# The head of a four-layer image kernel: moments of all samples in one run, weights loaded last and squared on GpSimd, bias sums under the last transpose, constant products on TensorE

## The chip, the cores and the metric

The kernel runs on one NeuronCore of a Trainium2 chip. The metric is device time in microseconds (us) of one execution; less is better. Below, PE is TensorE, DVE is VectorE, ACT is ScalarE, POOL is GpSimd, and SP is the engine whose queue issues most transfers. Everything is float32.

## The reference, cut to what matters

The input is four images of 56x56 pixels with 128 channels. Four layers follow one another, each as `x = x + layer(group_norm(x))`. The first layer is window attention followed by global attention and an MLP; the others (edge sums, a Fourier layer with attention, a convolution) are not touched here.

```
def _gn(v, G=32, eps=1e-5):
    ...
    m = jnp.mean(g, axis=(1, 2, 4), keepdims=True)
    s = jnp.var(g, axis=(1, 2, 4), keepdims=True)
    return ((g - m) / jnp.sqrt(s + eps)).reshape(v.shape)
...
x = x + _L0_conv_ref(_gn(x), L0_conv_wq, L0_conv_bq, ...)
```

Inside the first layer, attention is `softmax(q k / sqrt(32)) v`. A softmax needs the row's maximum only if scores can be large. The kernel therefore computes, before anything else, an upper bound for all scores from the longest normalized token and the norms of the weights' columns. If the bound is small, it takes a fast path without maxima; otherwise a general path. With the inputs given it takes the fast path.

## The kernel before, in words

Channels lie on the 128 partitions; a sample is a tile of 128x3136 (56x56 tokens), worked on in seven blocks of 448 tokens (`NBLK`, `NB`). This study concerns the head of the program, from the start to the branch `tc.If(small_scores > 0)` (L2868). The rest, some 3450 us, is the same in both versions.

**Loads.** SP issues eight transfers in the order sample 0 (`xw`), the pack `t_shared` (identity and the group matrix `g4`), samples 1 and 2 (`i_x`), the pack `t_first` (the first layer's weights), sample 3, the packs `t_edge` and `t_images` (L2829, L102).

**Moments.** `norm_steps` (L925) is a generator for one sample. Its first seven steps are one `bn_stats` each (L931, DVE). The eighth aggregates them (L934, `i_mv`) and multiplies by `g4` on PE (L936, into `i_ps`) to average over a group of four channels. The next step copies the mean (L940), forms the variance (L941, L942), multiplies by `g4` again (L943) and takes the root on ACT (L944). The last step inverts it on DVE (L946), forms the shift (L947), and squares the whole normalized sample on ACT in one instruction (L949, `i_sq`).

**Lengths.** `measure` inside `input_norms` (L954) multiplies the seven blocks of a sample's squares by a matrix of ones (L972), four blocks to a PSUM bank `i_len` (three banks in rotation), and reduces each full bank to a maximum per partition on DVE (L975, `i_tops`). At the end the maxima are reduced (L993, `i_top`), transposed on PE (L995, `i_pt`) and reduced to one number, `longest` (L996).

**Order.** Scheduling is by hand for PE, ACT and DVE: instructions stand in their queues as the Python code emits them. `input_norms` runs sample b's late steps in between the `bn_stats` of sample b+1, and calls `next(between)` once per sample, which advances a second generator: `score_bounds` (L999), then `attention_bias` (L899), then `edge_weights` (L1337). So `score_bounds` squares the weights `wq` and `wk` on DVE (`z_sq`, L1008 to L1011) and sums the squares' columns on PE (`z_p`, L1012 to L1015), all after sample 2's moments; scales and squares the sums (`z_both`, L1019 on DVE, L1020 on ACT) after sample 3's; and sums them by head (`z_norm`, L1026). `attention_bias` computes products of weights and shifts on PE (`b_p`, L905 to L909 and L920), scaled weights on DVE (`w_fq`, `w_fk`, `w_fv`, `w_f1`, L912), and adds biases (L916 to L922). They all stand ahead of the last sample's products.

**End of the head.** `scores_are_small` (L1031) combines `longest` and the norms into the flag `z_small`, which every engine loads (L1048) before it branches (L2868). Then POOL clears buffers (L339 to L345), ACT and DVE normalize the first groups of sample 0 (`w_xg`, L368 and L193), and PE projects them (L375, L376, L380), the results being copied out by L225, L223, L232, L230 and L383.

Elsewhere in the kernel (L1259, `e_idle`) PE already multiplies constants by constants, with a result that nobody reads.

Of the kernel before, what the change touches and what calls it, by code (L numbers as in the profile page):

```python
# [12 lines left out]
F32 = mybir.dt.float32  # L13
# [7 lines left out]
B = 4  # L21
# [76 lines left out]
def load_pack(k, pool, name, pack, owners):  # L98

    ap, places = pack  # L100
    t = pool.tile(list(ap.shape), F32, name="t_" + name)
    k.nc.sync.dma_start(t, ap)  # L102
    for n, shape, c in places:
        v = t[:shape[0], c:c + math.prod(shape[1:])]
        if len(shape) > 2:
            dims = ["d%d" % i for i in range(1, len(shape))]
            v = v.rearrange("p (%s) -> p %s" % (" ".join(dims), " ".join(dims)), **dict(zip(dims, shape[1:])))
        for prefix, owner in owners:
            if n.startswith(prefix):
                setattr(owner, n[len(prefix):], v)  # L110
# [788 lines left out]
def attention_bias(k, w, pool):  # L899


    nc = k.nc
    with k.tc.tile_pool(name="b_ps", bufs=1, space=PSUM) as psum:
        ps = psum.tile([P, 512], F32, name="b_p")
        nc.tensor.matmul(ps[:, 0:1], w.wo, w.bv, start=True, stop=True)  # L905
        for i, t in enumerate((w.wq, w.wk, w.wv)):
            nc.tensor.matmul(ps[:, 1 + i:2 + i], t, w.be1, start=True, stop=True)
        for f in range(4):
            nc.tensor.matmul(ps[:, 4 + f:5 + f], w.w1[:, f * P:(f + 1) * P], w.be2, start=True, stop=True)  # L909
        for n, t, g in (("fq", w.wq, w.g1), ("fk", w.wk, w.g1), ("fv", w.wv, w.g1), ("f1", w.w1, w.g2)):  # L910
            f = pool.tile(list(t.shape), F32, name="w_" + n)
            nc.vector.tensor_scalar_mul(f, t, g)  # L912
            setattr(w, n, f)
        for i, (n, bias) in enumerate((("bvo", w.bo), ("fbq", w.bq), ("fbk", w.bk), ("fbv", w.bv))):
            f = pool.tile([P, 1], F32, name="w_" + n)
            nc.vector.tensor_add(f, ps[:, i:i + 1], bias)  # L916
            setattr(w, n, f)
        w.fb1 = pool.tile([P, 4], F32, name="w_fb1")
        nc.vector.tensor_add(w.fb1, ps[:, 4:8], w.b1)
        nc.tensor.matmul(ps[:, 8:9], w.wo, w.fbv, start=True, stop=True)  # L920
        w.fbvo = pool.tile([P, 1], F32, name="w_fbvo")
        nc.vector.tensor_add(w.fbvo, ps[:, 8:9], w.bo)  # L922


def norm_steps(k, x, b, wk, psum):  # L925


    nc = k.nc
    st = wk.tile([P, NBLK, 6], F32, name="i_st")
    for j in range(NBLK):  # L930
        nc.vector.bn_stats(st[:, j, :], x[:, blk(j)])  # L931
        yield
    mv = wk.tile([P, 2], F32, name="i_mv")
    nc.vector.bn_aggr(mv, st.rearrange("p a b -> p (a b)"))  # L934
    ps = psum.tile([P, 512], F32, tag="mm", name="i_ps")
    nc.tensor.matmul(ps[:, 0:1], k.g4, mv[:, 0:1], start=True, stop=True)  # L936
    yield
    mr = k.mr[:, b, :]
    t = wk.tile([P, 2], F32, name="i_t")
    nc.vector.tensor_copy(mr[:, 0:1], ps[:, 0:1])  # L940
    nc.vector.tensor_sub(t[:, 0:1], mv[:, 0:1], mr[:, 0:1])  # L941
    nc.vector.scalar_tensor_tensor(t[:, 0:1], t[:, 0:1], t[:, 0:1], mv[:, 1:2], ALU.mult, ALU.add)  # L942
    nc.tensor.matmul(ps[:, 1:2], k.g4, t[:, 0:1], start=True, stop=True)  # L943
    nc.scalar.activation(t[:, 1:2], ps[:, 1:2], AF.Sqrt, bias=k.eps)  # L944
    yield
    nc.vector.reciprocal(mr[:, 1:2], t[:, 1:2])  # L946
    nc.vector.scalar_tensor_tensor(t[:, 0:1], mr[:, 0:1], -1.0, mr[:, 1:2], ALU.mult, ALU.mult)  # L947
    sq = wk.tile([P, TOK], F32, name="i_sq")
    nc.scalar.activation(sq, x, AF.Square, bias=t[:, 0:1], scale=mr[:, 1:2])  # L949
    k.squares[b] = sq  # L950
    yield


def input_norms(k, x, pool, wk, psum, between):  # L954

    nc = k.nc
    k.mr = pool.tile([P, B, 2], F32, name="mr0")
    k.longest = pool.tile([1, 1], F32, name="longest")  # L960
    k.squares = {}
    tops = wk.tile([P, NBLK], F32, name="i_tops", bufs=1)
    banks = {}

    def measure(b):
        sq = k.squares.pop(b)
        for j in range(NBLK):
            n = NBLK * b + j
            q = n % 4
            if q == 0:  # L970
                banks[n // 4] = psum.tile([P, 512], F32, tag="i_len", name="i_len", bufs=3)
            nc.tensor.matmul(banks[n // 4][32 * q:32 * q + 32, :NB], k.ones[:, 0:32], sq[:, blk(j)],  # L972
                             start=True, stop=True)
            if q == 3:
                nc.vector.tensor_reduce(tops[:, n // 4:n // 4 + 1], banks.pop(n // 4)[:, :NB], AX.X, ALU.max)  # L975

    steps = [norm_steps(k, x[b], b, wk, psum) for b in range(B)]
    for _ in range(NBLK + 1):
        next(steps[0])
    for b in range(B):  # L980
        ahead = steps[b + 1] if b + 1 < B else iter(())
        for n in range(NBLK + 1):
            next(ahead, None)
            if n in (1, 4):
                next(steps[b])
        next(between, None)
        if b:
            measure(b - 1)
    for _ in between:
        pass  # L990
    measure(B - 1)
    top = wk.tile([P, 1], F32, name="i_top", bufs=1)
    nc.vector.tensor_reduce(top, tops, AX.X, ALU.max)  # L993
    pt = psum.tile([P, 512], F32, tag="i_len", name="i_pt", bufs=3)
    nc.tensor.matmul(pt[0:1, :P], top, k.ident, start=True, stop=True)  # L995
    nc.vector.tensor_reduce(k.longest, pt[0:1, :P], AX.X, ALU.max)  # L996


def score_bounds(k, w, bounds, wk, psum, limits=(76.0, 64.0)):  # L999


    nc = k.nc
    ps = psum.tile([1, 2, 2, 2, P], F32, tag="z_p", name="z_p", bufs=1)
    for layer in range(2):
        for i, (wt, bias) in enumerate(((w.wq, w.bq), (w.wk, w.bk))):
            sq = wk.tile([P, P], F32, name="z_sq", bufs=4)
            if layer:
                nc.vector.tensor_scalar_mul(sq, wt, w.g1)  # L1008
                nc.vector.tensor_mul(sq, sq, sq)
            else:  # L1010
                nc.vector.tensor_mul(sq, wt, wt)  # L1011
            nc.tensor.matmul(ps[:, layer, i, 0, :], k.ones[:, 0:1], sq, start=True, stop=True)  # L1012
            if layer:
                nc.tensor.matmul(ps[:, layer, i, 1, :], w.be1, wt, start=True, stop=False)
            nc.tensor.matmul(ps[:, layer, i, 1, :], bias, k.ident, start=not layer, stop=True)  # L1015
    yield
    for layer in range(2):
        both = wk.tile([1, 2, 2, P], F32, name="z_both")
        nc.vector.tensor_scalar_mul(both[:, :, 0, :], ps[:, layer, :, 0, :], float(P) if layer else 1.0)  # L1019
        nc.scalar.activation(both[:, :, 1, :], ps[:, layer, :, 1, :], AF.Square)  # L1020
        bounds.append((both, limits[layer]))
    yield
    for layer in range(2):
        norm = wk.tile([1, 2, 2, 4], F32, name="z_norm%d" % layer, bufs=1)
        both, limit = bounds[layer]
        nc.vector.tensor_reduce(norm, both.rearrange("p i a (h d) -> p i a h d", h=4), AX.X, ALU.add)  # L1026
        bounds[layer] = norm, limit
    yield
# [308 lines left out]
def edge_weights(k, w, pool):  # L1337

    for n, t in (("nW2", w.W2), ("nbn", w.bn)):
        r = pool.tile(list(t.shape), F32, name="e_" + n)  # L1340
        k.nc.vector.tensor_scalar_mul(r, t, -1.0)
        setattr(w, n, r)
# [1455 lines left out]
def build(k, packs, I, out):  # L2798
# [3 lines left out]
    with ExitStack() as es:  # L2802
# [16 lines left out]
        with tc.tile_pool(name="w01", bufs=1) as wp, tc.tile_pool(name="io", bufs=1) as io:  # L2819
            xw = io.tile([P, TOK], F32, name="xw")  # L2820
            with ExitStack() as pre:
# [2 lines left out]
                w0, w1, w2 = Env(), Env(), Env()  # L2824
                owners = (("const_", k), ("in_w0_", w0), ("in_w1_", w1), ("in_w2_", w2))
                for b in range(B):
                    if b == 3:
                        load_pack(k, wp, "first", packs["first"], owners)
                    nc.sync.dma_start(x[b], I["x"][b])  # L2829
                    if b == 0:  # L2830
                        load_pack(k, cp, "shared", packs["shared"], owners)
                load_pack(k, wp, "edge", packs["edge"], owners)
                load_pack(k, l2p, "images", packs["images"], owners)
                make_consts(k, cp)
# [3 lines left out]
                                                              mybir.EngineType.DVE}))  # L2838
                bounds = []

                def between():
                    yield
                    yield from score_bounds(k, w0, bounds, wk, psum)
                    attention_bias(k, w0, wp)
                    edge_weights(k, w1, wp)

                input_norms(k, x, wp, wk, psum, between())
                k.shift = wp.tile([P, B], F32, name="shift0")
                nc.vector.scalar_tensor_tensor(k.shift, k.mr[:, :, 0], -1.0, k.mr[:, :, 1], ALU.mult, ALU.mult)
                small_scores = scores_are_small(k, bounds, wp, wk)  # L2850
# [102 lines left out]
```

## Time and profile before

| | us |
|---|---|
| median of 3 runs | 3492.82 |
| lowest and highest | 3477.65, 3494.12 |
| the profiled execution | 3507.88 |
| its span in the profile | 3505.9 |
| first work after the branch (`w_xg`, L368) begins | 52.92 |

| engine | busy us | share of the span |
|---|---|---|
| PE | 3342.7 | 95% |
| DVE | 2674.1 | 76% |
| ACT | 2130.6 | 61% |
| POOL | 1278.5 | 36% |

The profile is one execution, with a time of its own. A busy PE is not a PE at its peak, since the clock that it is granted varies; the page gives that clock by slice, and a window query gives it for any stretch. In the timeline a row is a start, a duration, an engine, a line of the program, the operation, its output and inputs, how many instructions are merged, and in brackets the idle time before it with what ended it. A float32 matmul shows as two records.

### The profile page before, as it was taken

The numbers are of one execution on the slowest core, as the hardware profiler recorded it, in microseconds if no ns is written. First come the engines' busy times: TensorE is split into PE (matmuls) and PEld (weight loads), VectorE is DVE, ScalarE is ACT, GpSimd is POOL, SyncE is SP. The second block draws the span as 40 slices with busy tenths as digits, with TensorE's granted clock in tenths as the row PEclk, the third lists the DMA queues.
The fourth block names the chain that finished last, engine by engine and source line by source line (L and its number), as shares of the span: only waits on it lengthen the run. The fifth ranks groups of instructions, "written<-read, shape, count | busy, mean of one in ns | idle before, by whom it ended". The sixth has DMA issues, their size and how long they took to land. (4 is left out here: it accounts for less than half of the span.)

```text
span 3505.9 us, 64398 instructions
## 1 busy us (share of the span) xinstructions
PE 3342.7 (95%) x27774; PEld 1447.5 (41%) x27774; DVE 2674.1 (76%) x2563; ACT 2130.6 (61%) x2251; POOL 1278.5 (36%) x784
## 2 busy tenths in 40 slices
PE   6999999999999999999999999999988999999998
PEld 4433333353333435333343543334346433336664
DVE  5588867868888696788859768885975778885766
ACT  4688876668888566788857578886642013215442
POOL 0000007700000590000029200001864778874776
PEclk8999999999999999999999999999998999999999
DMA  2134420023433000534400044332022047743201
GB/s 105 43 88 92 96 53 19 20 59 85 98 88 79 19 1 20 122 89 96 97 24 1 20 96 100 85 85 43 1 104 52 1 95 187 186 105 93 57 18 56
DMA packets 98014, 243.44 MB, mean 69 GB/s; under 512 B 64457, under 2 KB 69833, under 8 KB 92713
## 3 DMA queue, kind: packets, MB, share of 16 engines
q0 software_dynamic: 16128, 102.77, 14.7%
q1 hardware_dynamic: 74872, 123.61, 12.1%
q10 hardware_dynamic: 6720, 12.85, 1.3%
q8 instruction: 221, 3.62, 0.4%
q14 instruction: 73, 0.59, 0.1%
HBM read 79.43 MB, written 31.33 MB: 32 GB/s over the span
## 5 line engine op out<-in xcount | busy, mean ns | idle before, releaser
L830 ACT ACTIVATE f_ring<-f_pm 128x1792 f32<-128x1792 f32 (+1 forms) x764 | 1093.8, 1482 | 226.7 <-PE f_pm L827 179.7
L682 DVE TENSOR_TENSOR f_acc<-f_acc,f_ring 128x1792 f32<-128x1792 f32 x468 | 947.7, 2025 | 191.4 <-ACT f_ring L830 162.0
L827 PE MATMUL f_pm<-f_qT,f_kT 32*128 32x448 f32 x5376 | 723.0, 571 | 9.9 <-ACT f_p L716 4.1
L693 PE MATMUL f_pm<-f_ring,f_va 128*32 128x448 f32 (+1 forms) x6304 | 589.4, 490 | 0.0
L672 POOL DMA_DIRECT2D f_far<-f_ring x112 | 96.6, 862 | 1326.9 <-ACT f_ring L830 1071.8
L1230 POOL TENSOR_TENSOR e_tp<-e_a,e_c 128x1792 f32<-128x1792 f32 (+2 forms) x172 | 480.3, 2844 | 36.9 <-issue 36.9
L1228 DVE TENSOR_TENSOR e_td<-e_a,e_pc 128x1792 f32<-128x1792 f32 (+2 forms) x292 | 478.5, 1707 | 8.8 <-ACT e_c L1216 8.8
L827 PEld LDWEIGHTS f_pm<-f_qT,f_kT 32*128 32x128 f32 x5376 | 260.1, 183 | 412.0 <-ACT f_ring L830 300.8
L693 PEld LDWEIGHTS f_pm<-f_ring,f_va 128*32 128x32 f32 x6304 | 163.8, 109 | 410.1 <-issue 397.8
L1232 ACT ACTIVATE e_tp<-e_tp 128x1792 f32<-128x1792 f32 (+2 forms) x172 | 253.3, 1495 | 97.9 <-POOL e_tp L1230 97.9
L1979 DVE TENSOR_TENSOR u_ud<-u_px,u_d 112x1792 f32<-112x1792 f32 x144 | 263.5, 1864 | 39.8 <-PE u_po L1984 35.5
L1981 POOL TENSOR_TENSOR u_up<-xh,u_d 112x1792 f32<-112x1792 f32 (+1 forms) x72 | 241.0, 3375 | 55.2 <-PE u_po L1984 42.9
L1299 PE MATMUL e_acc<-e_td,t_edge 128*32 128x448 f32 x1952 | 231.6, 542 | 6.6 <-DVE e_td L1228 6.6
L1984 PE MATMUL u_po<-u_ud,AT 112*64 112x448 f32 x1056 | 213.8, 544 | 1.9 <-DVE u_ud L1979 1.9
L1299 PE MATMUL e_acc<-e_tp,t_edge 128*32 128x448 f32 x1184 | 147.9, 543 | 23.6 <-ACT e_tp L1232 23.6
L1984 PEld LDWEIGHTS u_po<-u_ud,AT 112*64 112x64 f32 x1056 | 74.5, 138 | 128.9 <-issue 112.9
L1299 PEld LDWEIGHTS e_acc<-e_td,t_edge 128*32 128x32 f32 x1952 | 61.7, 110 | 142.5 <-issue 93.8
L737 DVE RECIPROCAL f_den<-f_den 128x448 f32<-128x448 f32 x28 | 82.6, 2951 | 45.1 <-ACT f_den L734 45.1
L1823 POOL TENSOR_TENSOR q_u<-iS,q_g 128x1792 f32<-128x1792 f32 x32 | 102.8, 3235 | 28.4 <-PE q_acc L1838 28.4
L1838 PE MATMUL q_acc<-q_u,S 64*64 64x448 f32 x1024 | 106.5, 561 | 4.4 <-DVE q_u L1825 3.3
L813 POOL TENSOR_TENSOR x<-xf,xw 128x343 f32<-128x343 f32 x28 | 25.5, 910 | 226.5 <-DVE xf L802 226.5
L1984 PE MATMUL u_po<-u_up,AT 112*64 112x448 f32 x480 | 104.1, 547 | 2.4 <-POOL u_up L1981 2.4
(522 smaller groups left out, 4550.4 us busy)
## 6 DMA issues: line engine op xcount, KB each, us to landing
f_far<-f_ring POOLq DMA_DIRECT2D x112, 896.0 KB, 6.4
u_d<-dd SPq DMA_DIRECT2D x46, 784.0 KB
f_far<-f_ring SPq DMA_DIRECT2D x28, 896.0 KB
xw<-in_x SPq DMA_DIRECT2D x4, 1568.0 KB
x2d<-x SPq DMA_DIRECT2D x4, 1568.0 KB
xat<-x SPq DMA_DIRECT2D x4, 1568.0 KB
x_xs<-xat ACTq DMA_DIRECT2D x32, 196.0 KB
xm<-x_ev ACTq DMA_DIRECT2D x64, 98.0 KB
```

Source lines behind the costliest of these rows:

```text
L682: nc.vector.tensor_add(e.acc, e.acc, slots(j, c))
L693: nc.tensor.matmul(e.po[heads[h], part], va[o, c, heads[h]], p, start=(c == 0), stop=(c == 23 and part.stop == NB))
L827: nc.tensor.matmul(ss[:, i, :NB], kT[heads[h], c * P:(c + 1) * P], qT[heads[h], blk(j)], start=True, stop=True)
L830: nc.scalar.activation(ring[:, slot:slot + m, :], ss[:, :m, :NB], AF.Exp, scale=scale)
L1228: nc.vector.tensor_tensor(t, am, cm, ALU.max)
L1230: nc.gpsimd.tensor_sub(t, am, cm)
L1232: nc.scalar.activation(tf, tf, AF.Relu)
L1299: nc.tensor.matmul(acc[quarters[r0 + r], :NB], w.S[:, 0, :], t[:, r].rearrange("p l n -> p (l n)"), start=(g == 0), stop=(g == len(turns) ...
L1838: nc.tensor.matmul(acc[bp][i][halves[hb % 2], hb // 2, :NB], x[o], u[o, 8 * hb:8 * hb + 8, :].rearrange("p h t -> p (h t)"), start=first, ...
L1979: nc.vector.tensor_mul(u, bc(px[:, :, :NB], 2, m), dm)
L1981: nc.gpsimd.tensor_mul(u, bc(x, 2, m), dm)
L1984: nc.tensor.matmul(po[64 * b2:64 * b2 + 64, :NB], st.AT[:, 8 * i + h0 + q, 2 * bp + b2, :], u[:, b2, q, :], start=(left == 16), stop=(left ...
```

## The change

- The pack `t_first` is loaded after sample 3.
- `input_norms` no longer calls a generator between samples. The products of sample b-2 (`products`) are emitted inside the moments of sample b, and the reductions of their banks (`longest(b)`) are separate calls. The weights' work comes after sample 3's moments, in an order written out by hand. `z_p` is allocated at the beginning.
- `fill(n)` emits n products of a constant by a constant, 384 wide, into the bank of `z_p`: three inside sample 2's moments, three inside sample 3's, two before sample 3's second product, one after the last products, and four at the end.
- The squares of the weights (`z_sq`), the scaled weights `w_f*` and the squares in `z_both` are computed on POOL. The value that is squared in `z_both` is first copied from PSUM by DVE.
- The square of a sample is two ACT instructions, of four blocks and of three.
- `attention_bias` emits its `b_p` products and `w_f*` after the transpose of `i_top` has been emitted on PE, and its additions (now in `added`) before `longest` is reduced on DVE. Its PSUM pool is left open until then.

```diff
@@ attention_bias
-    with k.tc.tile_pool(name="b_ps", bufs=1, space=PSUM) as psum:
-        ps = psum.tile([P, 512], F32, name="b_p")
+    psum = k.tc.tile_pool(name="b_ps", bufs=1, space=PSUM)
+    ps = psum.__enter__().tile([P, 512], F32, name="b_p")
...
-            nc.vector.tensor_scalar_mul(f, t, g)
+            nc.gpsimd.tensor_scalar_mul(f, t, g)
             setattr(w, n, f)
+
+    def added():
...
+        psum.__exit__(None, None, None)
+
+    return added
@@ norm_steps
-    nc.scalar.activation(sq, x, AF.Square, bias=t[:, 0:1], scale=mr[:, 1:2])
+    for o in (slice(0, 4 * NB), slice(4 * NB, TOK)):
+        nc.scalar.activation(sq[:, o], x[:, o], AF.Square, bias=t[:, 0:1], scale=mr[:, 1:2])
@@ input_norms
+    ps = psum.tile([1, 2, 2, 2, P], F32, tag="z_p", name="z_p", bufs=1)
+
+    def fill(n):
+
+        for _ in range(n):
+            nc.tensor.matmul(ps[:, 0].rearrange("p i a c -> p (i a c)")[:, :3 * P], k.ones[:, 0:1], bc(k.ones, 1, 3),
+                             start=True, stop=True)
 
     steps = [norm_steps(k, x[b], b, wk, psum) for b in range(B)]
+    work = weights(ps)
     for _ in range(NBLK + 1):
         next(steps[0])
-    for b in range(B):
-        ahead = steps[b + 1] if b + 1 < B else iter(())
+    for b in range(1, B):
         for n in range(NBLK + 1):
-            next(ahead, None)
+            next(steps[b])
             if n in (1, 4):
-                next(steps[b])
-        next(between, None)
-        if b:
-            measure(b - 1)
-    for _ in between:
-        pass
-    measure(B - 1)
+                next(steps[b - 1])
+            if n == 5 and b > 1:
+                fill(3)
+                products(b - 2)
+            if n == 5 and b == 3:
+                next(work)
+        if b == 2:
+            longest(0)
+    longest(1)
+    fill(2)
+    next(steps[3])
+    next(steps[3])
+    products(2)
+    longest(2)
+    next(work)
+    next(work)
+    products(3)
+    next(work)
+    longest(3)
     top = wk.tile([P, 1], F32, name="i_top", bufs=1)
     nc.vector.tensor_reduce(top, tops, AX.X, ALU.max)
+    fill(1)
     pt = psum.tile([P, 512], F32, tag="i_len", name="i_pt", bufs=3)
     nc.tensor.matmul(pt[0:1, :P], top, k.ident, start=True, stop=True)
+    for _ in range(2):
+        next(work)
     nc.vector.tensor_reduce(k.longest, pt[0:1, :P], AX.X, ALU.max)
+    fill(4)
@@ score_bounds
-                nc.vector.tensor_scalar_mul(sq, wt, w.g1)
-                nc.vector.tensor_mul(sq, sq, sq)
+                nc.gpsimd.tensor_scalar_mul(sq, wt, w.g1)
+                nc.gpsimd.tensor_mul(sq, sq, sq)
             else:
-                nc.vector.tensor_mul(sq, wt, wt)
+                nc.gpsimd.tensor_mul(sq, wt, wt)
...
-        nc.scalar.activation(both[:, :, 1, :], ps[:, layer, :, 1, :], AF.Square)
+        nc.vector.tensor_copy(both[:, :, 1, :], ps[:, layer, :, 1, :])
+        nc.gpsimd.tensor_mul(both[:, :, 1, :], both[:, :, 1, :], both[:, :, 1, :])
@@ build
                 for b in range(B):
-                    if b == 3:
-                        load_pack(k, wp, "first", packs["first"], owners)
                     nc.sync.dma_start(x[b], I["x"][b])
...
+                load_pack(k, wp, "first", packs["first"], owners)
                 load_pack(k, wp, "edge", packs["edge"], owners)
...
-                def between():
+                def weights(ps):
+                    yield from score_bounds(k, w0, bounds, wk, ps)
+                    added = attention_bias(k, w0, wp)
+                    edge_weights(k, w1, wp)
                     yield
-                    yield from score_bounds(k, w0, bounds, wk, psum)
-                    attention_bias(k, w0, wp)
-                    edge_weights(k, w1, wp)
+                    added()
+                    yield
```

More of the change, by code (lines that the diff above doesn't have):

```diff
@@ L902, in attention_bias @@
     nc = k.nc
-    with k.tc.tile_pool(name="b_ps", bufs=1, space=PSUM) as psum:
-        ps = psum.tile([P, 512], F32, name="b_p")
+    psum = k.tc.tile_pool(name="b_ps", bufs=1, space=PSUM)
+    ps = psum.__enter__().tile([P, 512], F32, name="b_p")
+    if True:
         nc.tensor.matmul(ps[:, 0:1], w.wo, w.bv, start=True, stop=True)
@@ L948, in norm_steps, with input_norms @@
     sq = wk.tile([P, TOK], F32, name="i_sq")
-    nc.scalar.activation(sq, x, AF.Square, bias=t[:, 0:1], scale=mr[:, 1:2])
+    for o in (slice(0, 4 * NB), slice(4 * NB, TOK)):
+        nc.scalar.activation(sq[:, o], x[:, o], AF.Square, bias=t[:, 0:1], scale=mr[:, 1:2])
     k.squares[b] = sq
     yield
-def input_norms(k, x, pool, wk, psum, between):
+def input_norms(k, x, pool, wk, psum, weights):
     nc = k.nc
@@ L963, in input_norms, with products @@
     banks = {}
-    def measure(b):
+    def products(b):
         sq = k.squares.pop(b)
@@ L973, in measure, with longest @@
                              start=True, stop=True)
-            if q == 3:
-                nc.vector.tensor_reduce(tops[:, n // 4:n // 4 + 1], banks.pop(n // 4)[:, :NB], AX.X, ALU.max)
+    def longest(b):
+        for n in range(NBLK * b // 4, (NBLK * b + NBLK) // 4):
+            nc.vector.tensor_reduce(tops[:, n:n + 1], banks.pop(n)[:, :NB], AX.X, ALU.max)
+    ps = psum.tile([1, 2, 2, 2, P], F32, tag="z_p", name="z_p", bufs=1)
[3 more added lines that the diff above has]
+                             start=True, stop=True)
@@ L994, in input_norms, with score_bounds @@
     pt = psum.tile([P, 512], F32, tag="i_len", name="i_pt", bufs=3)
     nc.tensor.matmul(pt[0:1, :P], top, k.ident, start=True, stop=True)
+    for _ in range(2):
+        next(work)
     nc.vector.tensor_reduce(k.longest, pt[0:1, :P], AX.X, ALU.max)
-def score_bounds(k, w, bounds, wk, psum, limits=(76.0, 64.0)):
+    fill(4)
+def score_bounds(k, w, bounds, wk, ps, limits=(76.0, 64.0)):
     nc = k.nc
-    ps = psum.tile([1, 2, 2, 2, P], F32, tag="z_p", name="z_p", bufs=1)
+    squares = []
+    for layer in range(2):
+        for wt in (w.wq, w.wk):
+            sq = wk.tile([P, P], F32, name="z_sq", bufs=4)
+            if layer:
+                nc.gpsimd.tensor_scalar_mul(sq, wt, w.g1)
+                nc.gpsimd.tensor_mul(sq, sq, sq)
+            else:
+                nc.gpsimd.tensor_mul(sq, wt, wt)
+            squares.append(sq)
+    yield
@@ L1004, in score_bounds @@
     for layer in range(2):
         for i, (wt, bias) in enumerate(((w.wq, w.bq), (w.wk, w.bk))):
-            sq = wk.tile([P, P], F32, name="z_sq", bufs=4)
-            if layer:
-                nc.vector.tensor_scalar_mul(sq, wt, w.g1)
-                nc.vector.tensor_mul(sq, sq, sq)
-            else:
-                nc.vector.tensor_mul(sq, wt, wt)
+            sq = squares.pop(0)
             nc.tensor.matmul(ps[:, layer, i, 0, :], k.ones[:, 0:1], sq, start=True, stop=True)
@@ L2839, in build @@
                 bounds = []
-                def between():
+                def weights(ps):
+                    yield from score_bounds(k, w0, bounds, wk, ps)
+                    added = attention_bias(k, w0, wp)
+                    edge_weights(k, w1, wp)
                     yield
-                    yield from score_bounds(k, w0, bounds, wk, psum)
-                    attention_bias(k, w0, wp)
-                    edge_weights(k, w1, wp)
-                input_norms(k, x, wp, wk, psum, between())
+                    added()
+                    yield
+                input_norms(k, x, wp, wk, psum, weights)
                 k.shift = wp.tile([P, B], F32, name="shift0")
```

## The prediction, made before the changed kernel had run

> **What bounds the kernel now.** I read the page's 40 slices first: PE is at 9 nearly throughout, but at 6 in slice 1, and the granted clock dips there to 8. The page's chain explains only some 27% of the span and never reaches the start, so I read the first 53 us in order of time, then the waits, then 2-us windows for the clock.
>
> ```profile
> PE   6999999999999999999999999999988999999998
> PEclk8999999999999999999999999999998999999999
> ```
>
> The program cannot start sample 0 before `z_small` is known and the branch taken. First window work starts at 52.92. Timeline of that stage (start, duration, engine, line):
>
> ```profile
> 21.47 0.42 DVE L1011 TENSOR_TENSOR z_sq<-t_first 128x128 f32<-128x128 f32 x2
> ...
> 26.89 0.63 DVE L975 TENSOR_REDUCE i_tops<-i_len 128x1 f32<-128x448 f32 x1 [3.95 <-PE i_len L972]
> 27.44 1.14 DVE L931 BATCH_NORM_STATS2 i_st<-i_x 128x6 f32<-128x448 f32 x2
> ...
> 38.96 3.00 ACT L949 ACTIVATE i_sq<-i_x,i_t,mr 128x3136 f32<-128x3136 f32 x1 [0.50 <-DVE i_t L947]
> ...
> 42.89 1.85 PE L909 MATMUL b_p<-t_first 128*128 128x1 f32 x8
> ...
> 45.77 3.21 PE L972 MATMUL i_len<-i_sq,c_ones 128*32 128x448 f32 x14
> ...
> 50.41 0.28 DVE L996 TENSOR_REDUCE longest<-i_pt 1x1 f32<-1x128 f32 x1 [0.56 <-PE i_pt L995]
> ...
> 52.92 1.32 ACT L368 ACTIVATE w_xg<-xw,shift,mr 128x392 f32<-128x392 f32 x2 [1.62 <-DVE z_small L1047]
> ```
>
> To see: sample 3's moments (27.44) sit on DVE behind the weights' squares and a reduction that waits 3.95 us for PE; from there the chain is moments 3, square 3 (38.96), `b_p` on PE ahead of the last products, products (45.77), `longest`, branch.
>
> The clock column (seventh; PE's busy time comes first) shows how slowly PE runs here:
>
> ```profile
> 32.00:34.00 2.00, 1.40 (x10) 0.87 (x13) 1.01 (x4) 2.00 (x2) 0.00 (x0) 0.54 0.01 4
> 46.00:48.00 2.00, 2.00 (x11) 0.37 (x6) 0.69 (x4) 0.00 (x0) 0.00 (x0) 0.50 0.00 0
> 50.00:52.00 2.00, 0.38 (x2) 0.08 (x2) 1.20 (x8) 0.32 (x2) 0.00 (x0) 1.00 0.00 0
> 54.00:56.00 2.00, 2.00 (x4) 0.85 (x3) 1.18 (x2) 0.24 (x1) 2.00 (x6) 0.50 0.00 0
> 60.00:62.00 2.00, 2.00 (x26) 1.46 (x26) 1.32 (x4) 0.68 (x3) 1.43 (x7) 1.00 0.00 0
> ```
>
> From 32 to 49 it is half, then again from 53 to 59, when sample 0 starts. Seven products take 3.21 us so; the first set, at 25.68, took 1.88. (At 22 the column says 1.00, but `z_p` pairs come 0.43 apart and after 25.4 only 0.22: it was half until then.)
>
> [...] grants at 25.2, 49.2 and 59.3 follow dense starts at 22.2, 45.8 and 53.7, so 3.1 to 5.6 us. [...]1792 wide: 3.27 against 1.71[...] one-input 448 wide took 1.40 on POOL, 512 wide 0.48 on DVE. [...] Before, that load (L813) lay 28 us ahead of its first use[...].
>
> **The change, part by part.** Until 21.55 (moments 2) DVE, ACT and their DMAs stay as they are.
>
> *Loads.* SP issues as many DMAs, `t_first` third from last. By the windows' GB/s, 7.40 MB have moved at 19.9; the first sample's statistics ran some 1.1 after its last byte, so `t_first` is usable at about 21.0, `t_edge` at 22.8, x3 at 19.0. Users: POOL at 21.0, DVE's `e_nW` after 40. Nothing waits that matters.
>
> *To POOL.* Off DVE go six `z_sq` instructions (1.5 us) and four `w_f*` (1.3); off ACT two squares (0.62). On POOL, from L2062 (112 wide, 0.418), L813 (343, 0.910), L1744 (64, 0.442) and L1715 (448, 1.406): 128-wide two-input 0.45, one-input 0.60, 512-wide 1.57. Squares 4x0.45+2x0.60=3.0, so 21.0 to 24.0[...]; `w_f*` 3.4 more. PE wants `z_sq` at 34.9: [...] later than that, each us is one on the path. `w_f*` is read by L468 at 115. The two `z_both` squares (0.72 each) now pass DVE, POOL, DVE: +0.5 us on the path to the last reductions.
>
> *Constant products.* 3+3+2+1+4=13. `e_idle` at 684.34 (four 384-wide records in 1.45, the last 0.49 long) gives 0.32 a record, 0.64 a matmul at full clock; cold is twice that, as `z_p` shows. So three cost 1.9 to 3.85 us, ahead of the real products and of moments 2 and 3's small matmuls, L942 and L949, in PE's queue. They write the bank of `z_p` before its sums start; only the one after products 3 waits, for `z_both` to be read (37.8 below), and that is past.
>
> *Halved Square.* 1792 wide took 1.70 (L1232), 1344 wide 1.29 (L830): 3.0 together; I charge 0.05. It helps only if PE would wait for sample 3, and by my sum it doesn't.
>
> *Sum.* Fill 18.85 to 22.7, cold. Clock granted between 22.0 and 24.5 (3.1 to 5.6 after start); I take 23.2. Products 0: first bank 24.0, all 24.9. DVE idles from 21.55 for that bank, reduces to 24.7, then two of x3's statistics to 25.9, copy and two small ops to 26.4, three statistics. Before, that triple started at 29.00 and square 2 began 2.05 later, moments 3 were aggregated 3.45 later: now square 2 28.55 to 31.6, moments 3 at 29.95, against 32.45. **2.5 us.** PE: L949 to 27.05, fill to 28.97, products 1 (1.88) to 30.85, L942 to 31.3, fill (2) to 32.6, L949 to 33.0. Square 3 follows by 0.8: 33.85 to 36.9. Before 38.96: **5.1 us**; the gain there is PE at full clock. Products 2 to 34.9, ten `z_p` (0.215) to 37.05, products 3 to 38.95. DVE meanwhile: two reductions to 35.2, `z_both` to 37.8, POOL to 38.6, norms to 39.3, last reductions to 40.55, `i_top` 40.7, against 49.85: **9.1 us**, of which `b_p` (4.6 on PE before) is only postponed.
>
> *`b_p` under the transpose.* `longest` now stands on DVE behind eight instructions, six waiting for `b_p` or its last product. Transpose to 41.2; nine weight loads: eight `b_p` cost 0.46 each cold (1.42 for three), 0.25 at full clock (loads of 128 took 190 ns a record in L1259): 2.0 to 3.7, I take 2.3 as the clock has few products to hold it: 43.5. Adds, L923, `w_fbvo`: 1.26 before, 1.35 here with waits: 44.85. From `longest` to first work took 2.51: 47.4 against 52.92, **5.5 us**. Ends: `b_p` cold and grant late, 49.4, 3.5 us; all early, 46, 7 us.
>
> *Sample 0's start.* Four fills at 44.6 to 47.2 end before L375 (48.2): PE starts at full clock. L375 to L380 took 4.9 us cold, 2.5 at full clock. But evacuations on DVE and ACT (four of 0.6, then two copies) hold most: the copy into `w_vd` comes 1 to 1.6 us sooner. I take 1.2. If the clock is lost in the thin 40-to-44 stretch, four fills last 5.1 and PE may stand until 50: 0 then, and with all of it favourable 2.
>
> Total: 5.5+1.2=**6.7 us less** (2 to 9). From there on each engine has the same instructions in the same order, so the shift should carry to the end. The profiled execution took 3507.88 (span 3505.9 and 2 around it): 3501.2. It lies 0.4% above the median of the three runs, so for those: 3492.8-6.7=**3486**.
>
> **Rivals.**
> (a) The clock doesn't come, slower. L991 stands in PE's queue ahead of L942 and L949. Cold throughout: fill and products 0 to 25.9, moments 3 at 31.2, fill and products 1 to 34.9, square 3 at 39.6, products 2, `z_p` and products 3 to 49.4, `b_p` to 54.7, first work 58.5, last fill to 60.7. PE starts 7 us later: 3500. It decides if no grant comes by about 31, that is after 12 us of dense products; every dense stretch before got it within 5.6.
> (b) A larger gain: full clock throughout, and sample 0 doesn't stall on evacuation: 9 to 10 us, 3483. For it, PE is the busiest engine in each 20-us window from 60 to 120 (19.4 and 20.0); against it, the 0.65 us pauses between DVE and ACT.
> (c) The fills gain nothing: PE cold again where it counts and only moved instructions pay, about 2 us: 3491. The 0.4 us of PE work in 49 to 52.5 did not hold the clock before.
> (d) Later stages shift by more than the head does (POOL's library load moved, another phase of transfers). Order and waits are the same, so I see no price beyond the spread.
>
> **Numbers.** Forecast 0.70, (a) 0.05, (b) 0.10, (c) 0.10, (d) 0.05 split both ways. 0.5% (17.5 us) is about what a measurement of this kernel can tell from no change; no mechanism here reaches it, only the runs' spread (-15 to +1 about the median) with the gain on top: faster 0.10, same 0.86, slower 0.04. Range: the runs shown less 2 to 9 give 3469 to 3492; (a) and (c) stretch the top: 3471 to 3497.
>
> **What would show it.** Right: first `w_xg` near 47.4 (46 to 49.4); x3's statistics start near 24.8; square 3 near 33.9; clock 1.00 from about 24 to 60; `z_sq` on POOL done before 31; PE at full clock in the first L375. Wrong: first work after 52, the clock at half beyond 27, DVE waiting on POOL for over 1 us before L1065, or the span beyond 60 us changed by more than the head.

## The result, and the profile after

| | before | after |
|---|---|---|
| median of 9 runs each, us | 3494.12 (3477.65 to 3501.14) | 3464.29 (3462.19 to 3470.79) |
| the profiled execution, us | 3507.88 | 3464.84 |
| its span, us | 3505.9 | 3463.1 |

The ratio is 0.9917, 95% interval 0.9899 to 0.9935: 29.8 us less, where the prediction had 6.7 less. In the page's two rows that carried the reading of before, the dips of slices 30 and 31 are gone, and so is the clock's in slice 1, where PE is at 7 instead of 6:

```profile
PE   7999999999999999999999999999999999999998
PEclk9999999999999999999999999999999999999999
```

The head ran almost as worked out. Its timeline after (start, duration, engine, line, operation):

```profile
21.09 0.75 POOL L1044 TENSOR_TENSOR z_sq<-t_first 128x128 f32<-128x128 f32 x2 [20.20 <-DMA t_first<-pack_first]
...
23.96 0.62 DVE L984 TENSOR_REDUCE i_tops<-i_len 128x1 f32<-128x448 f32 x1 [2.39 <-PE i_len L979]
...
24.50 1.14 DVE L937 BATCH_NORM_STATS2 i_st<-i_x 128x6 f32<-128x448 f32 x2
...
34.90 3.28 ACT L956 ACTIVATE i_sq<-i_x,i_t,mr 128x1792 f32<-128x1792 f32 x2 [0.50 <-DVE i_t L953]
...
42.65 1.03 PE L910 MATMUL b_p<-t_first 128*128 128x1 f32 x8
...
44.71 5.28 PE L991 MATMUL z_p<-c_ones 128*1 128x384 f32 x8
...
44.89 0.27 DVE L1028 TENSOR_REDUCE longest<-i_pt 1x1 f32<-1x128 f32 x1
...
47.45 1.32 ACT L368 ACTIVATE w_xg<-xw,shift,mr 128x392 f32<-128x392 f32 x2 [1.68 <-DVE z_small L1086]
...
50.14 1.14 PE L375 MATMUL w_mm<-w_xg,t_first 128*128 128x392 f32 x2
```

To see: squares of weights on POOL at 21.09, statistics of sample 3 at 24.50, `b_p` below the transpose, first `w_xg` at 47.45. But the last fill takes 5.28 us and sample 0's first product waits behind it to 50.14. The windows say why (the clock is the number ahead of the DMA share): it is back to half from 44, as it was from 28 to 30.

```profile
28.00:30.00 2.00, 2.00 (x10) 0.76 (x12) 1.62 (x5) 1.65 (x1) 0.00 (x0) 0.50 0.01 4
...
32.00:34.00 2.00, 2.00 (x13) 0.84 (x14) 0.55 (x4) 0.00 (x0) 0.00 (x0) 1.00 0.00 0
...
44.00:46.00 2.00, 1.80 (x5) 0.76 (x6) 1.01 (x10) 0.32 (x2) 0.00 (x0) 0.50 0.00 0
46.00:48.00 2.00, 2.00 (x5) 0.45 (x4) 1.14 (x6) 0.55 (x1) 0.48 (x2) 0.50 0.00 0
...
54.00:56.00 2.00, 2.00 (x14) 1.13 (x16) 1.11 (x2) 1.47 (x3) 1.87 (x8) 1.00 0.00 0
```

So far 5 us. I then lined up the two executions' instructions of each engine from the end and read how far after is ahead of before: 5.0 us from 75 to 684, 6.5, 7.6 and 9.1 past the three sample boundaries, **31.3 at 2725**, 32.2 at 3190, 42.9 at the end. The largest step, 22 us, lies between 2596 and 2725, in the last image's stage, which nothing in the diff touches. PE's waits from 2560 to 2760, before (total, times, longest, in us):

```profile
PE s_px L1654 <- DVE xh L232: 5.2, 1, 5.2
PE q_acc L1838 <- DVE q_u L1825: 3.3, 1, 3.3
PE q_pg L1849 <- issue: 3.0, 1, 3.0
PE s_pr L1616 <- issue: 2.5, 1, 2.5
```

and after:

```profile
PE q_pt L1919 <- DVE y L1911: 5.9, 1, 5.9
PE q_acc L1877 <- DVE q_u L1864: 3.3, 1, 3.3
PE e_acc L1338 <- DVE e_td L1267: 1.6, 4, 1.0
```

Two waits on "issue" (PE waits for nothing that the profile shows) and one on DVE are gone. Before, on PE's timeline, the first lies behind the first two records of a dense run of small products:

```profile
2601.24 0.27 PE L1616 MATMUL s_pr<-t_images,s_x 128*64 128x33 f32 x2 [0.60 <-DMA s_x<-xad]
2604.04 4.74 PE L1616 MATMUL s_pr<-t_images,s_x 128*64 128x33 f32 x110 [2.53 <-issue]
```

At `q_pg` it is the same, 122 products into a run of 134:

```profile
2705.36 2.02 PE L1849 MATMUL q_pg<-R 64*64 64x56 f32 x122
2710.37 0.39 PE L1849 MATMUL q_pg<-R 64*64 64x56 f32 x11 [2.99 <-issue]
```

In the trace's records the queue of instruction fetches (q8) reads 16 KB at 2601.62, for 0.91 us, and at 2707.81, for 1.22 us. These reads begin 0.1 and 0.4 us after PE has stopped, and PE resumes 1.5 and 1.3 us after their ends.

```profile
q8 instruction: 221, 3.62, 0.4%
```

That row is from the page before: 221 reads. Between two of them PE starts 254 matmuls and weight loads (median of 220 intervals; 256 with the other instructions in PE's queue); PE has 55,548 of the page's 64,398 instructions. The changed kernel has 13 products more in the head, which are 26 PE and 26 PEld records: 52 instructions that lie ahead of everything later.

A count settles where PE stops. I numbered PE's records of each trace from 0, those of its queue included. In before, PE resumes from the two waits at records 42,569 and 45,385, which are 2816 apart, eleven times 256. Seven of the kernels in this document, before among them, have waits on issue of 1.9 us or more at `s_pr` or `q_pg`, 13 in all; in each the record at which PE resumes has a number 72 or 73 above a multiple of 256.

### The profile page after: what moved, and what is told of

The parts are those of the page before. It is cut to its first block, busy times and chain, and to the rows that moved or that the text cites. A ratio compares the mean times of both kernels' runs of the same rounds, so it can differ in the third digit from the quotient of the medians.

```text
span 3463.1 us, 64456 instructions
## 1 busy us (share of the span) xinstructions
PE 3319.0 (96%) x27800; PEld 1425.6 (41%) x27800; DVE 2657.9 (77%) x2555; ACT 2131.1 (62%) x2253; POOL 1285.9 (37%) x796
## 5 line engine op out<-in xcount | busy, mean ns | idle before, releaser
L2020 POOL TENSOR_TENSOR u_up<-xh,u_d 112x1792 f32<-112x1792 f32 (+1 forms) x72 | 240.9, 3373 | 55.0 <-PE u_po L2023 40.7
L813 POOL TENSOR_TENSOR x<-xf,xw 128x343 f32<-128x343 f32 x28 | 25.5, 911 | 224.7 <-DVE xf L802 224.7
L2121 ACT COPY x_ev<-x_po 56x896 f32<-56x896 f32 x32 | 28.8, 900 | 126.9 <-DMA x_xs<-xat 51.1
```

Of the source, the lines that this page charges most:

```text
L2020: nc.gpsimd.tensor_mul(u, bc(x, 2, m), dm)
```

## The experiments

Four theories went into the first group. **Fetch:** the 13 products move every later PE instruction against the borders of the blocks (a block is what q8 reads at a time: 16 KB, 256 of PE's instructions at the median). **Port** (only a name: no run shows what POOL and DVE share): POOL's operations in the head change how POOL and DVE collide later. **Shift:** starting 5 us earlier matters. **Chance:** the clock falls otherwise each time. The ratios stand against runs of the kernel before on the same chip: median 3488.13 (55 runs) in the first group, 3492.4 (49) in the second, 3486.82 (43) in the third.

**The changed kernel again (e1_after), no edit.**

> The changed kernel again, nothing edited. Four theories of the 24 us that the head does not explain. Fetch: the 13 more PE products move every later PE instruction against the blocks in which instructions are fetched. Port: the POOL library load and POOL's operations in the head change how POOL and DVE collide later. Shift: only the 5 us by which everything later starts earlier matters. [...] Fetch, port and shift: the ratio is again 0.990 to 0.993, and a new profile has again 1.1 us in the w_xg of DVE (L193) at the three sample boundaries, no wait on issue over 1 us at s_pr and q_pg between 2596 and 2725, and no half clock there beyond the first 7 us. Chance: one or two of these are back, and the profiled time is 10 us or more from 3465.

3464.29 us, ratio 0.9936 (0.9919 to 0.9953), a shade above the range given. PE's waits are the same, with one on issue of 1.2 at `s_pt` instead; one of the three boundaries had 3.6 us in `w_xg` and not 1.1. Chance does not make the gain.

**The kernel before with 13 small products where PE is idle (e1_before_pe13).**

```diff
     banks = {}
+    pad = psum.tile([1, 2, 2, 2, P], F32, tag="z_p", name="z_pad", bufs=1)
+    for _ in range(13):
+        nc.tensor.matmul(pad[:, 0, 0, 0, 0:8], k.ones[:, 0:1], k.ones[:, 0:8], start=True, stop=True)
```

> The kernel before with 13 products of 8 columns in PE's first idle time (from 1 us; PE's first real work is at 11.9), so that PE has as many more instructions as in the changed kernel and the head takes the same time. Fetch: the waits on issue at s_pr and q_pg vanish or move, the stretch from 2596 to 2725 takes 20 us less, and the time is 3465 to 3478. Port, shift: no change, ratio 0.998 to 1.002 (3488 to 3501). Chance: anything between 3475 and 3500, with other stretches at half clock.

3466.52 us, ratio 0.9948 (0.9928 to 0.9967). The products ran from 1.07 to 1.87, with PE idle until 11.77. So 0.8 us of idle time filled with products that nobody reads takes 21.6 us off. The run of `s_pr` that was cut in two before is whole:

```profile
2595.70 3.46 PE L1619 MATMUL s_pr<-t_images,s_x 128*64 128x33 f32 x112 [1.01 <-DMA s_x<-xad]
```

**The kernel before with one POOL product in the head (e1_before_pool).**

```diff
+    early = wk.tile([P, P], F32, name="early", bufs=1)
+    nc.gpsimd.tensor_mul(early, k.ident, k.ident)
```

> The kernel before with one product of 128 columns on POOL in the head, which nobody reads: POOL's library load moves from sample 0's last blocks to the head, as in the changed kernel. Port: the w_xg of DVE at the boundaries falls from 3.6 to 1.1 us and the 784-wide x at 2631 from 13.3 to some 3.5 us, 5 us for the boundaries and 10 to 17 us for the other, 3470 to 3480. Fetch on PE, shift: no change, ratio 0.998 to 1.002. Chance: between 3475 and 3500.

3484.05 us, ratio 0.9993 (0.9976 to 1.0009). The waits of before are back (s_px 5.1, q_pg 2.5, s_pr 2.7), and DVE's `x` took 13.28 us. Moving POOL's library load (my name for the record MODIFY_POOL_CONFIG, in before at 476.7) from L813 to the head does nothing that can be measured. But the kernel before loads a second time, at L1746, at 2596.40 and so at the start of the very stage; e1_before_pool still does, at 2590.54, and the changed kernel doesn't. Other runs rule this load out: e1_before_pe13 has it (2590.76) and is quick, e3_after_pe51 below hasn't and is slow.

**The changed kernel without its fills (e1_after_nofill):** `range(n)` in `fill` becomes `range(0 * n)`.

> The changed kernel without its 13 constant products; everything else is as changed. The head: PE cold for longer, so that first work starts some 2 us later than 47.4 by the prediction's rival (49 to 51). Fetch: PE's instructions lie again as before, the 20 us between 2596 and 2725 come back, 3484 to 3492. Port: they stay away, and only the head's 2 us are lost, 3465 to 3469. Shift: the later stages start 2 us later than in the changed kernel and 3 earlier than before; between the two.

3476.26 us, ratio 0.9968 (0.9954 to 0.9982): 12 us of the gain are lost, and yet first work starts at 45.5, earlier than with the fills. The head was expected to be later (49 to 51). PE's waits:

```profile
PE q_pg L1888 <- issue: 4.5, 1, 4.5
...
PE s_pr L1655 <- issue: 1.9, 1, 1.9
```

The waits are where fetch has them, but the time lies 8 us below its range (3484 to 3492), between those of fetch and port, where shift had it: DVE's `x` took 1.6 us at most here, not 13.3. Shift does not explain it, since first work is earlier than in the changed kernel and the waits are back.

Fetch stands, port (in the form of the library load), shift and chance fall as causes of the gain. The second group tests fetch by the size of a block, and takes up DVE's long instruction.

**64 and 32 small products (e2_before_pe64, e2_before_pe32):** `range(64)` and `range(32)` in the edit above, 256 and 128 PE instructions.

> The kernel before with 64 products of 8 columns at 1 us, 256 PE instructions; they take some 4 us of PE's idle time until 11.9, so the head stays. The queue of instruction fetches reads blocks of 16 KB, one for about every 252 PE instructions in the trace. Block theory (what counts is where the block borders fall in the dense products of the last image's stage): 256 more is a whole block, so the borders fall as before: waits on issue of 2 to 3 us at s_pr and at q_pg are back, 3478 to 3490. Rival (any added product wakes PE, or delays nothing but shifts it, and the gain of 13 was from that): as with 13, 3464 to 3468, no such waits.

3489.33 us, ratio 0.9995 (0.9978 to 1.0013). Both waits are back, after one or two `s_pr` as before:

```profile
PE q_pg L1852 <- issue: 2.9, 1, 2.9
PE s_pr L1619 <- issue: 2.9, 1, 2.9
```

> The kernel before with 32 such products, 128 PE instructions, half a block. Block theory: the two waits on issue vanish at these places or turn up at other instructions of the dense stretch; no more than one of over 1.5 us, 3464 to 3480. Rival (any added product does it): 3464 to 3468.

3474.72 us, ratio 0.9961 (0.9943 to 0.9979); in the stage one wait on issue, of 0.9 us at `s_pr`. The effect has the period of a block: 0 and 256 instructions are slow, 52 and 128 quick. This is what shows that borders count. (In this profiled execution 10 us went later, in two stretches at half clock from 3171 and 3297 on. The profile before has the like at 3203 and 3329, e1_before_pool has neither, though PE's list is the same.)

So a block is 16 KB by q8's records, and 256 of PE's instructions by the median between two reads, by the count of the waits and by this period. In before, from 2570 to 2740, two crossings took 2.5 and 3.0 us of PE; at the fourteen others by that count PE's records start at most 0.3 us apart.

**The last image's normalization on ACT instead of DVE (e2_before_act).**

```diff
+        if b == B - 1:
+            sh = wk.tile([P, 1], F32, name="s_shift", bufs=1)
+            nc.vector.scalar_tensor_tensor(sh, mr[:, 0:1], -1.0, mr[:, 1:2], ALU.mult, ALU.mult)
         for t in range(0, HH, 14):
-            apply_norm(k, x[:, t:t + 14, :], x[:, t:t + 14, :], mr)
+            if b == B - 1:
+                nc.scalar.activation(x[:, t:t + 14, :], x[:, t:t + 14, :], AF.Identity, bias=sh, scale=mr[:, 1:2])
+            else:
+                apply_norm(k, x[:, t:t + 14, :], x[:, t:t + 14, :], mr)
```

The reason lies in the timeline before, of DVE and then of POOL, which issues without a gap:

```profile
2630.96 13.27 DVE L193 TENSOR_SCALAR x<-x,s_mr 128x784 f32<-128x784 f32 x1
2644.15 0.60 DVE L232 COPY xh<-s_px 112x448 f32<-112x448 f32 x1
```

```profile
2630.03 1.41 POOL L1715 TENSOR_SCALAR d_m<-t_w_V,t_images 128x448 f32<-128x448 f32 x1
2631.42 1.25 POOL L1757 TENSOR_TENSOR q_g<-q_g,q_t 128x512 f32<-128x512 f32 x1
```

> The kernel before with the last image's normalization (x<-x,s_mr, four of 784 wide, L193) on ACT instead of DVE; PE's instructions are untouched. Port theory: the 13.3 us that the first of them took on DVE beside POOL's back-to-back operations is gone; s_px no longer waits 5 us for DVE; 8 to 13 us less than before, 3475 to 3481, while the waits on issue at s_pr and q_pg stay. Rival (PE's waits on issue cost it all, DVE's long instruction lies beside them): no change, 3485 to 3491.

3488.78 us, ratio 0.9998 (0.998 to 1.0017): the rival's time, but not for its reason. The four pieces took 1.04 us each on ACT. But then another DVE instruction with one input stood long, 128x56, which takes 0.25 in e1_after_nofill:

```profile
2631.86 7.93 DVE L1603 TENSOR_SCALAR norm<-s_d,t_images 128x56 f32<-128x56 f32 x1
```

and PE waited 5.5 us for DVE at `s_ps`. The delay moved to another instruction, and the time stayed. The waits on issue stayed too, 2.1 us at `s_pr` and 3.3 at `q_pg`.

**The changed kernel with the number but not the work of its fills (e2_after_nofill_pe13, again as e3_after_nofill_pe13, beside e3_after).** `fill` does nothing, and the 13 small products stand at 1 us.

> The changed kernel with its 13 constant products of 384 columns in the head taken out, and 13 of 8 columns put in at 1 us instead, so that PE has as many instructions as in the changed kernel. The last trace without them had first work at 45.5 against 47.4, 2.5 us ahead by 75 us. If the fills only cost, and what they brought is the number of instructions: 3460 to 3463, no waits on issue at s_pr and q_pg. If their work in the head is what keeps the later stages quick: 3474 to 3480, as without them.

3462.91 us, ratio 0.9917 (0.989 to 0.9944); first work at 46.4.

> The changed kernel once more, beside the next two on one chip. 3463 to 3466, ratio 0.990 to 0.994 whatever the theory.

3465.27 us, 0.994 (0.9915 to 0.9964).

> The changed kernel without the fills' work and with its number of PE instructions, again, for a narrow comparison. If the fills' work only costs: 1 to 2.5 us below the changed kernel, 3461.5 to 3463.5. If the earlier gap was chance: within 0.5 us of it.

3460.65 us, 0.9924 (0.9901 to 0.9947), 0.9 below the range given; first work at 45.9, first L375 at 46.70. On one chip it is 4.6 us below the changed kernel (six runs of each, 3459.3 to 3463.4 against 3463.5 to 3474.3). It beats both kernels. The fills' work costs; their number pays.

**The changed kernel with 51 small products more (e3_after_pe51):** the edit of e1_before_pe13 with `range(51)`, in the changed kernel; 13 and 51 make a block.

> The changed kernel, all of it, with 51 products of 8 columns more at 1 us: with its own 13 that makes 64, a whole block of PE instructions against the kernel before. Block theory: the waits on issue at s_pr and q_pg are back as before, and most of the gain is gone though the head is as changed: 3474 to 3486. Rival (the changed head's order and POOL operations made the later gain): 3463 to 3467.

3483.64 us, ratio 0.9989 (0.9974 to 1.0003). First work is at 47.5, as changed, and the gain is gone:

```profile
PE q_pg L1890 <- issue: 3.0, 1, 3.0
PE s_pr L1657 <- issue: 3.0, 1, 3.0
```

**The 13 small products behind the first wait and ahead of the second (e3_before_late13).**

```diff
                     spectra(k, w2, st, xat, images)
+                    with tc.tile_pool(name="pad_ps", bufs=1, space=PSUM) as pp:
+                        pad = pp.tile([P, 512], F32, name="z_pad")
+                        for _ in range(13):
+                            nc.tensor.matmul(pad[0:1, 0:8], k.ones[:, 0:1], k.ones[:, 0:8], start=True, stop=True)
```

> The kernel before with the 13 products of 8 columns not in the head but behind the last s_px, right ahead of q_acc, some 2690 us in: after the wait at s_pr and before the one at q_pg. Block theory, read at its place: the wait on issue at s_pr (2.5 us) and DVE's long x beside POOL stay, the wait at q_pg (3.0) goes; 2 to 6 us less than before, 3483 to 3489. Rival (the length of the whole program, and so where it lies in memory, counts, not the place): as with 13 in the head, 3464 to 3468.

3479.33 us, ratio 0.9982 (0.997 to 0.9995). PE's list has

```profile
PE s_pr L1616 <- issue: 2.3, 1, 2.3
```

and no wait at `q_pg`. That fits the place, not the program's length. The time came out 4 us below the range given. Against the trace before, which its DVE matches to 0.2 us from 1350 to 2621, some 8 us went where DVE's `x` took 4.7 instead of 13.3 us, and 5 around `q_pg`. That `x` would take as long as before was wrong.

The stage in one number, from the first `s_pr` to the first `q_pt` (their rows give the first starts, 2601.2 and 2778.3 for before):

| kernel | PE instructions more | us | waits on issue, `s_pr` and `q_pg` |
|---|---|---|---|
| before | 0 | 177.1 | 2.5, 3.0 |
| e1_before_pool | 0 | 174.7 | 2.7, 2.5 |
| e1_after_nofill | 0 | 165.9 | 1.9, 4.5 |
| e2_before_act | 0 | 174.8 | 2.1, 3.3 |
| e2_before_pe64 | 256 | 175.3 | 2.9, 2.9 |
| e3_after_pe51 | 256 | 177.2 | 3.0, 3.0 |
| e3_before_late13 | 52 for `q_pg` alone | 164.3 | 2.3, none |
| e1_before_pe13 | 52 | 154.3 | none |
| after, e1_after, e3_after | 52 | 155.3, 155.1, 151.5 | none |
| e2_after_nofill_pe13, e3_after_nofill_pe13 | 52 | 155.2, 153.4 | none; 0.3 at `s_pr` |
| e2_before_pe32 | 128 | 152.0 | 0.9 at `s_pr` |

## Why the prediction was wrong

- **The failed step** is "From there on each engine has the same instructions in the same order, so the shift should carry to the end", and with it rival (d)'s "Order and waits are the same, so I see no price beyond the spread". The order was the same, the place of PE's instructions in their blocks was not. That the span beyond 60 us changed by more than the head is a sign of being wrong that the prediction named itself; of the causes that (d) names for it, POOL's library load is ruled out by the runs above. The fills were costed by PE's time alone; that they are also 52 entries ahead of all later ones was left out, and this is most of the gain: 21.6 us by the kernel before with 13 small products, 12.0 by the changed kernel with and without fills.
- **How 5.5 us of waiting became some 20.** Of the 21.8 us by which the stage is shorter in the trace after, 5.5 are the two waits. The rest follows them. Between 2570 and 2770 the clock was at half for 30.7 us before and for 17.1 after, in the clock's records; 13.6 us at half are an estimated 6.8 of work. And DVE's first `x` took 13.27 us before and 0.68 after, with 5.2 us of PE's time behind it. Together that is 17.5; 4.3 us I can't place. POOL started eighteen instructions in those 13.27 us, without a gap; that POOL held DVE is my reading, and no run shows by what. That the clock and `x` follow from the waits is shown only as far as both go when the border is moved. e1_after_nofill parts them a little: with both waits and `x` not held (1.6 us at most) its stage takes 165.9 us, against 151.5 to 155.3 without the waits and 174.7 to 177.2 with the waits and a held instruction (7.9 to 13.3 us).
- **Right:** the steps of the head. Predicted and measured: statistics of sample 3 at 24.8 and 24.50, square 3 at 33.9 and 34.90, `i_top` at 40.7 and 41.12, `b_p` to 43.5 and 43.68, first work at 47.4 and 47.45; `z_sq` on POOL at 21.0 and 21.09. The squares of the weights were done on POOL by 23.74 (24.0 in the sum); POOL's library load, at 0.8, lay 20 us ahead of the first of them. The halved square cost 0.28 (3.28 against 3.00), not 0.05.
- **The clock in the head** was not as forecast, full from about 24 to 60. In its records it is full from 23.33, at half from 26.74 to 30.16, full to 43.81 and at half to 50.64; half beyond 27 was one of the prediction's signs of being wrong. (The three grants of before that the prediction reckons from are at 25.34, 49.24 and 59.48 in the records, 3.1, 3.4 and 5.8 us after the starts that it gives.) Square 3 and `i_top` came 1.0 and 0.4 us late, and the path from `i_top` to first work was 0.4 shorter than the sum (6.33 against 6.7). That 47.45 meets 47.4 so closely is luck; e1_after had 46.8.
- **Two readings of the trace before** fell short. The prediction's 1.71 us on DVE, for two inputs of 1792 columns (L1228), is a mean over several shapes; that shape alone took 2.01, so POOL's 3.27 (L1230) is 1.6 times as long. And beside the load 28 us ahead of its first use there was one right ahead of it: L1746, loaded at 2596.40, started at 2596.52 and took 0.37.
- **Sample 0's start**, 1.2 us of the sum, was 0: the gain fell from 5.5 to 5.0 by 75 us. The last fill ran cold, the case that the text gave as "PE may stand until 50". L375 began at 50.14, 2.7 us after first work. Without fills it began 0.8 after, at half clock, and the first group's products were through at 50.7 all the same, against 53.0.
- **What the fills do for the head** was misjudged in rival (c), which gave 2 us to the moved work alone. Without fills first work comes at 45.5 to 46.4, against 46.8 to 47.5 with them. The moved instructions made the head's gain, and the fills took some back: the transpose of `i_top` began at 39.01 in e3_after_nofill_pe13 and at 41.42 with the fills, which stand ahead of the real products in PE's queue.
- **The head's base.** 52.9 was one of two values: with before's head, first work lies at 49.8 to 50.2 in four profiles and at 52.9 to 53.6 in three. So the 5.5 us are 2.4 or more by the other value. With 13 products more in both, the medians of the first group put the changed head at 2.2 us (3466.52 to 3464.29).
- **The range and the chances** took the spread of before as given. Most of it hung on the borders too: in the first group the kernel before took 3474.6 to 3502.6, and with 13 small products more 11 of its 13 runs lie between 3463.8 and 3467.9.

Left open: the 10 us at 3203 and 3329 and the 1 to 1.6 us at the sample boundaries, where L193 took 3.6 us in some executions, and 1.1 and 2.1 in a pair of instructions in others of one kernel; what decides whether DVE is held (`x` took 4.7 to 13.3 us in five kernels), as it was not in e1_after_nofill (1.6 us), with both waits on issue there; and why PE stops at these two borders and not at others. That PE used up instructions faster than they were read would fit `q_pg`, where the 256 records ahead of the border took 2.55 us, but not `s_pr`, where they took 23.0 and the run had just begun; further borders in the runs of `s_pr` (6.7 us for 256 records) were crossed without a wait.

## What to carry to other kernels

In a run of small products PE can stop where a block of instructions ends, here for 1.9 to 4.5 us at 13 such places, and where the block borders fall is set by the number of instructions ahead on that engine: 52 more moved both waits away, 256 more left them where they were. So an edit to one stage is to be compared with a dummy of as many instructions before its gain or loss is put down to its work; and with waits on "issue" in such a run, a few idle instructions in a free place ahead of it are a cheap thing to try. Constant products for the clock's sake stand in PE's queue ahead of real ones; here that cost more than the clock brought (3465.27 with them, 3460.65 with their number alone).

## What the runs showed of the hardware

PE's run of `q_pg` starts 134 products and as many weight loads in 2.15 us, so it uses up 256 instructions, a block, in an estimated 2.05 us (2.15 for 268):

```profile
2681.97 2.15 PE L1852 MATMUL q_pg<-R 64*64 64x56 f32 x134
```

That row is from e1_before_pe13. A border at `s_pr` or `q_pg` stopped PE for 1.9 to 4.5 us in seven kernels, always at the same count of instructions modulo 256, and in before PE resumed 1.5 and 1.3 us after the end of a 16 KB read on the instruction queue. A DVE instruction with one input, of 0.25 or 0.68 us, stood for 4.7 to 13.3 us beside POOL operations without gaps. How long differs between kernels that have the same order on both engines: 13.27 us in before, 8.98 in e2_before_pe64, 4.69 in e3_before_late13.
